# Softmax sums of every second j tile added up by accumulating DMAs, with one product with ones for them, in a four-layer graph network kernel

## The chip, the cores and the metric

The kernel runs on one core of a Trainium2 chip. The metric is device microseconds for one execution, and a time is the median of several runs. Times of the trace come from one further execution, taken with the hardware profiler. Engines are named as the profile names them: PE is the matrix engine (PEld its weight loads), DVE the vector engine, ACT the activation engine, POOL the GpSimd engine, SP the engine that issues nearly all DMAs.

## What is computed

Four layers over `x` of shape (8, 2048, 128), with one adjacency matrix of 2048 x 2048 for all. Layers 0 and 3 are graph attention with one head, layer 2 is a mean over neighbours. The change lies in layer 1, masked attention with four heads of 32:

```python
q = (x @ W_q).reshape(Bn, Nn, NUM_HEADS, HEAD_DIM).transpose(0, 2, 1, 3)
...
scores = jnp.einsum('bhnd,bhmd->bhnm', q, k) / np.sqrt(HEAD_DIM).astype(np.float32)
scores = jnp.where(adj == 0, -jnp.inf, scores)
attn = jax.nn.softmax(scores, axis=-1)
out = jnp.einsum('bhnm,bhmd->bhnd', attn, v)
out = out.transpose(0, 2, 1, 3).reshape(Bn, Nn, NUM_HEADS * HEAD_DIM)
return out @ W_o + b_o
```

The kernel does not divide the weights. It forms e = exp(score + shift) x mask, sums e x v and e alone over all j, and divides at the end. The sums of e alone are the "softmax sums" of the title.

## The kernel before

**Tiles of the attention.** Columns of a weight tile are 256 targets i, its partitions 128 sources j. A block is (b, ib, jp): batch b of 8, one of 8 groups of 256 targets, one of 8 pairs of j tiles; 512 blocks in all, jp innermost. A block goes through four functions:

- `scores` (L1017): for each of its 2 j tiles and 4 heads, one product of 32 x 128 keys with 32 x 256 queries, into two PSUM tiles. A float32 product is two instructions on PE, so the trace shows 16 a block.
- `exponentials` (L1035): two ACT instructions over 1,024 elements a partition write the tile `e`, laid out as head, j tile, target. `e` comes from the pool `ep` with 4 buffers of 8 KB a partition.
- `masked_weights` (L1043): two DVE instructions multiply `e` by the 0/1 mask in place.
- `values` (L1053): for each j tile, four products (one a head, in its own 32 columns of PE) of the values with `e` into `acc[:, 0, :]`, and four of a tile of ones with `e` into `acc[:, 1, :]`. Both sums accumulate in PSUM over the 16 j tiles of a (b, ib). L1063 is the line of both.

After jp = 7, `finished` (L1072) takes the reciprocal of `acc[:, 1, :]` (L1079), multiplies (L1081) and goes through `wo`.

**Order.** PE, DVE, ACT and POOL run in the order in which the program issues instructions. `block_steps` gives each block six steps: scores in step 0, exponentials in step 1, loads ahead in step 2, masks in step 3. In step 0 of block n, after its scores, come the values of block n-2. These steps are the main list. Other work is woven between them: by `work`, in proportion to given weights, and by `locked`, which sets three main steps beside each step of a graph attention loop. The other work is layer 0 of a batch ahead, layers 2 and 3 of the batch behind, and the norms and projections before the attention. So the distance from one block to the next differs from stretch to stretch.

**POOL's queue.** POOL has the roots of the norms (L356, L357), which DVE or ACT wait for when they apply a norm (L364, L372, L379), the node weights (L606), and the scaling of the graph attention's values (`gat_values`, L496, four steps of four instructions each). It issues no DMA before the change.

**SP's queue.** SP issues the loads in program order: masks `mh` of the attention (512 KB each, L1011), keys, values and queries (L1001, L1003, L1007), masks and rows of the graph attentions (L508, L517), x, and stores. A DMA that has to wait for a buffer or for its data holds back those behind it.

**Adjacency tiles.** Before the attention, `load_adj` (L1166) takes its 16 tiles of 1 MB from the pool `ep` too; `neighbours` (L1177) reads one and then loads the one four tiles on.

Of the kernel before, what the change touches and what calls it, by code (L numbers as in the profile page):

```python
# [15 lines left out]
AF = mybir.ActivationFunctionType  # L16
ALU = mybir.AluOpType
AX = mybir.AxisListType

P = 128  # L20
# [13 lines left out]
NH = 4  # L34
HD = 32
# [3 lines left out]
def fast_path(  # L39
# [34 lines left out]
    nc = tc.nc  # L74
    B, N, F = x.shape
    T = N // P
# [3 lines left out]
    def pool(name, bufs, **kw):  # L80
        return ctx.enter_context(tc.tile_pool(name=name, bufs=bufs, **kw))
# [2 lines left out]
    xp = pool("xp", 12)  # L84
    kp = pool("kp", 6)
    qp = pool("qp", 2)
    ep = pool("ep", 4)
    op = pool("op", 1)
    mp = pool("mp", 3)
    mtp = pool("mtp", 3)  # L90
# [17 lines left out]
    def new(pool_, tag, s, shape, dt=F32):  # L108
        count[0] += 1
        return pool_.tile(list(shape), dt, tag=tag, name=f"{s}_{count[0]}")  # L110
# [58 lines left out]
    ones = const.tile([P, HD], F32, name="ones")  # L169
# [25 lines left out]
    def load_row(name, ap):  # L195
# [21 lines left out]
        out=rows[2 * T + 2 : 2 * T + 4], in_=a3.rearrange("(c f) o -> c (f o)", c=2)  # L217
# [374 lines left out]
    def layer0_ahead(b, eng=nc.gpsimd):  # L592
# [73 lines left out]
        for g in range(G):  # L666
            steps.add(0.3, lambda g=g: values(g))
# [31 lines left out]
    attn, ready, shifts = {}, {}, {}  # L699
# [226 lines left out]
    def layer3(b):  # L926
# [43 lines left out]
        for g in range(G):  # L970
            pre.add(0.3, lambda g=g: values(g))
# [41 lines left out]
    IB, JP = N // 256, T // 2  # L1013
    blocks = [(b, ib, jp) for b in range(B) for ib in range(IB) for jp in range(JP)]
    SUB = 6

    def scores(blk):  # L1017

        b, ib, jp = blk["at"]
        c0 = (ib % 2) * 256  # L1020
        blk["sc"] = psum("sc", (P, 2, 2, 256), n=2)
        held[0] += 2
        for c in range(2):
            j = 2 * jp + c
            for h in range(NH):
                r = slice(h * HD, (h + 1) * HD)
                nc.tensor.matmul(  # L1027
                    blk["sc"][h // 2][:, h % 2, c, :],
                    keys[b, j // 4][r, (j % 4) * P : (j % 4 + 1) * P],
                    queries[b, ib // 2][r, c0 : c0 + 256],  # L1030
                    start=True,
                    stop=True,
                )

    def exponentials(blk):  # L1035
        e = blk["e"] = new(ep, "e", "e", (P, NH, 2, 256))
        for a in range(2):
            nc.scalar.activation(  # L1038
                e[:, 2 * a : 2 * a + 2], blk["sc"][a], AF.Exp, bias=shifts[blk["at"][0]]
            )  # L1040
        held[0] -= 2

    def masked_weights(blk):  # L1043
        b, ib, jp = blk["at"]
        c0 = (ib % 2) * 256
        k = 2 * jp % 8
        m = masks[b, ib // 2, jp // 4][:, k : k + 2, c0 : c0 + 256]
        m = m.unsqueeze(1).to_broadcast([P, 2, 2, 256])
        for a in range(2):
            e = blk["e"][:, 2 * a : 2 * a + 2]  # L1050
            nc.vector.tensor_tensor(e, e, m, ALU.mult)  # L1051

    def values(blk):  # L1053
        b, ib, jp = blk["at"]
        if jp == 0:
            state["acc"] = new(psa, "acc", "acc", (P, 2, 256))
        acc = state["acc"]
        for c in range(2):
            j = 2 * jp + c
            for s in range(2):  # L1060
                for h in range(NH):
                    r = slice(h * HD, (h + 1) * HD)
                    nc.tensor.matmul(  # L1063
                        acc[r, s, :],
                        ones if s else vals[b, j // 4][:, j % 4, r],
                        blk["e"][:, h, c, :],
                        start=(j == 0 and s == 0),
                        stop=(j == T - 1),
                        skip_group_check=True,
                    )  # L1070

    def finished(blk):  # L1072

        b, ib, _ = blk["at"]
        acc, ao = state.pop("acc"), {}

        def weigh():
            ao["rec"] = new(op, "rec", "rec", (P, 256))
            nc.vector.reciprocal(ao["rec"], acc[:, 1, :])  # L1079
            ao["T"] = new(op, "aoT", "aoT", (P, 256))  # L1080
            nc.vector.tensor_tensor(ao["T"], acc[:, 0, :], ao["rec"], ALU.mult)  # L1081

        def measured():
            k = b * IB + ib
            nc.scalar.activation(
                ao["rec"], ao["rec"], AF.Copy, accum_out=sums[:, k : k + 1]
            )

        def back():
            pw = psum("pwo", (P, 2, P))  # L1090
            for t in range(2):
                nc.tensor.matmul(
                    pw[:, t, :], ao["T"][:, t * P : (t + 1) * P], wo, start=True, stop=True
                )
            k = 2 * (ib % 2)
            xg = xs[b][ib // 2][:, k : k + 2, :]
            ao["last"] = later(lambda: nc.vector.tensor_tensor(xg, pw, xg, ALU.add))

        def wait():
            pass  # L1100

        return [weigh, measured] + [wait] * 5 + [back, wait, wait, lambda: settle(ao["last"])]

    def prefetch(n):
        b, ib, jp = blocks[n]
        g = ib // 2
        if n == 0:
            for k in range(G):
                load_keys(0, k)
            load_queries(0, 0)  # L1110
            for k in range(2):
                load_masks(0, 0, k)
        nb, ng = (b, g + 1) if g + 1 < G else (b + 1, 0)
        if ib % 2 == 1 and nb < B:
            if jp == 2:
                load_masks(nb, ng, 0)
                load_queries(nb, ng)
            if jp == 5:
                load_masks(nb, ng, 1)
            if nb > b:  # L1120
                if jp == 2:
                    load_keys(nb, 0)
                if jp >= 2 and jp % 2 == 0:
                    load_keys(nb, jp // 2)

    state = {}
    going = {}

    def block_steps(n):

        blk = {}

        def sub(s):
            def go():
                if s == 0:
                    if n < len(blocks):
                        if n == 0:
                            prefetch(0)
                        blk["at"] = blocks[n]
                        going[n] = blk  # L1140
                        scores(blk)
                    if n >= 2 and n - 2 < len(blocks):
                        old = going.pop(n - 2)
                        values(old)
                        if old["at"][2] == JP - 1:
                            pending.extend(finished(old))
                elif s == 1 and n < len(blocks):
                    exponentials(blk)
                elif s == 2 and 0 < n < len(blocks):
                    prefetch(n)  # L1150
                elif s == 3 and n < len(blocks):
                    masked_weights(blk)
                if pending:
                    pending.pop(0)()

            return go

        return [sub(s) for s in range(SUB)]
# [84 lines left out]
    with tc.manual_schedule(engines=ENGINES):  # L1243
# [10 lines left out]
        n = 12  # L1254
# [107 lines left out]
        for b in range(B):  # L1362
# [10 lines left out]
            if b + 1 < B:  # L1373
                xs[b + 1] = []
                loop0 = layer0_loop(b + 1, sts[b + 1])
                n = -6 if b else len(side)
# [6 lines left out]
                if loop3:  # L1383
# [4 lines left out]
                    n = len(loop0) - 4  # L1388
# [320 lines left out]
def gnn_kernel(tc, x, *others):  # L1709

    nc = tc.nc
    B, N, F = x.shape
    T, G = N // P, N // 512
    with ExitStack() as ctx:
        dr = ctx.enter_context(tc.tile_pool(name="dr", bufs=1, space=bass.MemoryType.DRAM))
        fl = ctx.enter_context(tc.tile_pool(name="fl", bufs=1))

        mt_all = [dr.tile([P, T, 512], FP8, tag=f"mt{g}", name=f"mt_all{g}") for g in range(G)]
        mg_all = [
            dr.tile([P, T, n * P], FP8, tag=f"mg{k}", name=f"mg_all{k}")  # L1720
            for k, (_, n) in enumerate(GROUPS)
        ]
        dv_all = dr.tile([T, P], F32, tag="dv", name="dv_all")
        hb_all = [dr.tile([P, 4, P], F32, tag=f"hb{g}", name=f"hb_all{g}") for g in range(G)]
        kept = (mt_all, mg_all, dv_all, hb_all)
        within = fl.tile([P, 2 * B], F32, name="within")
        flag = fl.tile([1, 1], F32, name="flag")
        fast_path(tc, kept, within, flag, x, *others)
        least = fl.tile([1, 1], F32, name="least")
        nc.vector.tensor_reduce(least, within[0:1, :], AX.X, ALU.min)  # L1730
        nc.vector.tensor_tensor(least, least, flag, ALU.min)
        usual = fl.tile([1, 1], I32, name="usual")
        nc.vector.tensor_copy(usual, least)
        v = nc.values_load(usual[0:1, 0:1], min_val=0, max_val=1)
        with tc.If(v == 0):
            general_path(tc, kept, x, *others)
# [52 lines left out]
```

## Time and profile before

| | us |
|---|---|
| median of 3 runs (3563.13 to 3566.41) | 3564.96 |
| the profiled execution | 3572.35 |
| its span, first to last instruction | 3570.5 |
| first and last start of L1063 | 216.9 to 3415.1 |
| DVE before its masks, idle until ACT's exponentials (209 times) | 304.1 |
| ACT before its exponentials, idle until PE's scores (326 times) | 452.9 |
| PE before its scores, idle until ACT's exponentials (8 times) | 14.1 |
| POOL before L356, idle until DVE's statistics (101 times) | 1486.6 |

Mean granted TensorE clock 0.962; DMA 82 GB/s on average. In the page, a group's row gives the line, the engine, the operation, output and inputs by name, the shapes and the count; behind the bar stand the busy time, the mean of one in ns, and the engine's idle time just before with what ended it. PE's busy time is modelled, and the four heads of a group run beside each other in PE's columns, so a mean of one product is longer than its share of the time. The chain of waits is followed back from the last instruction, at each step to what released it. A timeline row gives start, duration, engine, line and a run of like instructions.

### The profile page before, as it was taken

The page shows a single profiled execution, that of the slowest core. Times are in us where ns is not written, and L with a number is a line of the kernel's source. Part 1 is how long each engine was busy: PE and PEld are TensorE (multiplying, and loading weights), DVE is VectorE, ACT ScalarE, POOL GpSimd, SP SyncE. Part 2 cuts the span into 40 slices and gives each one's busy share as a digit, 9 for nine tenths or more (in the row PEclk, how much of TensorE's full clock was granted, in tenths as well). Part 3 has the DMA queues.
Part 4 walks back from the last instruction along what each step waited for, and adds up shares of the span by engine and source line. Part 5 has one row for each costly group of instructions (what it writes and reads, how often), then busy time and mean ns, then how long its engine had stood idle before and what let it go on. Part 6 is the DMA issues. An engine that isn't in the chain of part 4 may idle for free.

```text
span 3570.5 us, 85981 instructions
## 1 busy us (share of the span) xinstructions
PE 3253.6 (91%) x36367; PEld 2339.9 (66%) x36367; DVE 2684.5 (75%) x4933; ACT 2596.0 (73%) x3969; POOL 774.8 (22%) x717
## 2 busy tenths in 40 slices
PE   4789988999999999999999999999999999999987
PEld 3656654676766766676766767577676776655767
DVE  6668767677867878588795787768785887857755
ACT  4667756777876778777877687767787677676766
POOL 1032023111431115113241023311142120103011
PEclk7989988999999999999999999999999999999989
DMA  8511121213231132311323132221323112130132
GB/s 295 169 57 56 38 89 50 86 46 109 70 103 54 47 114 83 105 39 57 105 78 102 47 102 71 91 69 49 116 69 115 41 52 94 59 105 31 47 111 59
DMA packets 185190, 292.91 MB, mean 82 GB/s; under 512 B 36647, under 2 KB 99805, under 8 KB 182749
## 3 DMA queue, kind: packets, MB, share of 16 engines
q1 hardware_dynamic: 184288, 287.12, 25.4%
q8 instruction: 288, 4.72, 0.5%
q14 instruction: 106, 0.86, 0.1%
q10 hardware_dynamic: 508, 0.22, 0.0%
HBM read 235.75 MB, written 51.52 MB: 80 GB/s over the span
## 4 chain that ended last, share of the span: by engine, by line
PE 58%; DVE 27%; ACT 10%; issue 3%; POOL 1%; DMA 1%; SPq 0%; ACTq 0%; DVEq 0%; POOLq 0%
PE gacc L548 17%; PE acc L1063 17%; PE sc L1027 11%; DVE e L1051 9%; PE pagg L869 7%; DVE ge L537 5%; ACT ge L532 3%; ACT e L1038 3%; DVE ln_s L348 2%; DVE rec L1079 2%; DVE h L364 2%; ACT h L379 1%; PE ptr L390 1%; PE pqk L724 1%; PE ph L404 1%
## 5 line engine op out<-in xcount | busy, mean ns | idle before, releaser
L1051 DVE TENSOR_TENSOR e<-e,mh 128x1024 f32<-128x1024 f32 x1024 | 1208.6, 1222 | 304.3 <-ACT e L1038 304.1
L1038 ACT ACTIVATE e<-sc,shift 128x1024 f32<-128x1024 f32 x1024 | 1082.8, 1109 | 457.4 <-PE sc L1027 452.9
L548 PE MATMUL gacc<-va,ge 128*128 128x129 f32 x8192 | 1040.4, 281 | 127.7 <-DVE ge L537 66.4
L548 PEld LDWEIGHTS gacc<-va,ge 128*128 128x128 f32 x8192 | 966.7, 194 | 257.5 <-issue 140.8
L532 ACT ACTIVATE ge<-ab,gnf,gt 128x384 f32<-128x384 f32 (+1 forms) x1536 | 905.8, 666 | 27.6 <-DMA ab<-rowd 19.3
L537 DVE SCALAR_TENSOR_TENSOR ge<-ge,gnf,mg 128x768 f32<-128x768 f32 (+1 forms) x768 | 692.8, 931 | 47.1 <-ACT ge L532 40.0
L1027 PE MATMUL sc<-qr,ks 32*128 32x256 f32 x8192 | 650.5, 412 | 65.0 <-ACT e L1038 14.1
L1063 PE MATMUL acc<-e,vs 128*32 128x256 f32 x8192 | 663.9, 396 | 6.8 <-DVE aoT L1081 5.7
L1063 PE MATMUL acc<-e,ones 128*32 128x256 f32 x8192 | 649.3, 389 | 0.0
L1027 PEld LDWEIGHTS sc<-qr,ks 32*128 32x128 f32 x8192 | 403.3, 188 | 193.8 <-issue 41.8
L356 POOL TENSOR_SCALAR ln_r<-ln_mv 128x4 f32<-128x4 f32 x128 | 117.9, 921 | 1494.4 <-DVE ln_mv L350 1486.6
L1063 PEld LDWEIGHTS acc<-e,vs 128*32 128x32 f32 x8192 | 219.2, 111 | 280.2 <-issue 179.3
L1063 PEld LDWEIGHTS acc<-e,ones 128*32 128x32 f32 x8192 | 273.2, 113 | 188.5 <-issue 20.8
L860 ACT CAST mr<-mt 128x512 fp32r<-128x512 fp8e4 x512 | 272.2, 619 | 48.3 <-PE pagg L869 45.5
L869 PE MATMUL pagg<-mr,hm 128*128 128x512 f32 x1024 | 259.0, 407 | 12.2 <-ACT mr L860 6.8
L869 PEld LDWEIGHTS pagg<-mr,hm 128*128 128x128 f32 x1024 | 180.3, 190 | 86.0 <-ACT mr L860 45.3
L357 POOL TENSOR_TENSOR ln_r<-ln_r,neg_half 128x4 f32<-128x4 f32 x128 | 208.5, 1629 | 10.7
L1079 DVE RECIPROCAL rec<-acc 128x256 f32<-128x256 f32 x64 | 112.3, 1755 | 108.5 <-PE acc L1063 108.5
L493 POOL COPY va<-gv 128x16 f32<-128x16 f32 x15 | 3.2, 213 | 733.4 <-ACT gv L471 733.4
L889 DVE TENSOR_TENSOR agT<-pagg,dv 128x512 f32<-128x512 f32 x32 | 22.1, 691 | 158.8 <-PE pagg L869 151.0
L496 POOL TENSOR_SCALAR va<-va,gv 128x128 f32<-128x128 f32 x128 | 133.9, 1065 | 0.0
L390 PE MATMUL ptr<-ident,h 128*128 128x128 f32 x512 | 92.2, 300 | 42.8 <-DVE h L364 30.6
(168 smaller groups left out, 2273.9 us busy)
## 6 DMA issues: line engine op xcount, KB each, us to landing
mg<-mg_all SPq DMA_DIRECT2D x128, 384.0 KB, 3.2
mh<-mt_all SPq DMA_DIRECT2D x64, 512.0 KB, 3.8
mt<-mt_all SPq DMA_DIRECT2D x64, 512.0 KB, 3.9
adj<-in_adj_dram SPq DMA_DIRECT2D x16, 1024.0 KB, 7.8
mg<-mg_all SPq DMA_DIRECT2D x64, 256.0 KB, 2.9
ab<-rowd SPq DMA_DIRECT2D x64, 192.0 KB, 3.2
h<-in_x_dram SPq DMA_DIRECT2D x32, 256.0 KB, 3.0
x<-in_x_dram SPq DMA_DIRECT2D x32, 256.0 KB, 2.9
```

The source lines that it names most:

```text
L357: nc.gpsimd.tensor_tensor(r, r, neg_half[:, 0:4], ALU.pow)
L496: eng.tensor_scalar(va[:, j, 0:P], h[:, k, :], st["v"][:, j : j + 1], None, ALU.mult)
L532: nc.scalar.activation(e[:, c, :], gr[k]["rho"], AF.Relu, bias=st["nf"], scale=t)
L537: nc.vector.scalar_tensor_tensor(e, e, st["nf"], mt, ALU.subtract, ALU.mult)
L548: nc.tensor.matmul(gr[k]["acc"][:, q, :], e[:, c, q * P : (q + 1) * P], st["va"][:, j, :], start=(j == 0 and q == 0), stop=(j == T - 1), s ...
L860: nc.scalar.copy(t, st["mt", g, j // 8][:, j % 8, :])
L869: nc.tensor.matmul(st["pa"], st["hm"][:, j, s, :], m, start=(j == 0 and s == 0), stop=(j == T - 1 and s == 1), skip_group_check=True,)
L1027: nc.tensor.matmul(blk["sc"][h // 2][:, h % 2, c, :], keys[b, j // 4][r, (j % 4) * P : (j % 4 + 1) * P], queries[b, ib // 2][r, c0 : c0 + ...
L1038: nc.scalar.activation(e[:, 2 * a : 2 * a + 2], blk["sc"][a], AF.Exp, bias=shifts[blk["at"][0]])
L1051: nc.vector.tensor_tensor(e, e, m, ALU.mult)
L1063: nc.tensor.matmul(acc[r, s, :], ones if s else vals[b, j // 4][:, j % 4, r], blk["e"][:, h, c, :], start=(j == 0 and s == 0), stop=(j == ...
L1079: nc.vector.reciprocal(ao["rec"], acc[:, 1, :])
```

## The change

The tile `e` is laid out as j tile, head, target, so that one j tile's four heads are 4 KB in one piece on each partition. For the blocks with jp below 7, the second j tile's weights no longer meet the ones on PE. A new function adds them, after the mask, into one SBUF tile a (b, ib): SP copies the first, and for jp 1 to 6 POOL issues DMAs that add to the tile. In the block with jp = 7 both j tiles still meet the ones, and after them four products of ones with the added-up tile close the sum. A new pool `sp` holds two such tiles of 4 KB a partition, and `ep` has 3 buffers in place of 4. The new function is called in step 5 of each block.

```diff
-    ep = pool("ep", 4)
+    ep = pool("ep", 3)
+    sp = pool("sp", 2)
...
     def exponentials(blk):
-        e = blk["e"] = new(ep, "e", "e", (P, NH, 2, 256))
+        e = blk["e"] = new(ep, "e", "e", (P, 2, NH, 256))
         for a in range(2):
             nc.scalar.activation(
-                e[:, 2 * a : 2 * a + 2], blk["sc"][a], AF.Exp, bias=shifts[blk["at"][0]]
+                e[:, :, 2 * a : 2 * a + 2, :].rearrange("p c h i -> p h c i"),
+                blk["sc"][a], AF.Exp, bias=shifts[blk["at"][0]],
             )
...
-        m = m.unsqueeze(1).to_broadcast([P, 2, 2, 256])
+        m = m.unsqueeze(2).to_broadcast([P, 2, 2, 256])
         for a in range(2):
-            e = blk["e"][:, 2 * a : 2 * a + 2]
+            e = blk["e"][:, :, 2 * a : 2 * a + 2, :]
             nc.vector.tensor_tensor(e, e, m, ALU.mult)
+
+    def added(blk):
+        b, ib, jp = blk["at"]
+        if jp == JP - 1:
+            return
+        e = blk["e"][:, 1].rearrange("p h i -> p (h i)")
+        if jp == 0:
+            adds[b, ib] = new(sp, "adds", "adds", (P, NH * 256))
+            nc.sync.dma_start(out=adds[b, ib], in_=e)
+        else:
+            nc.gpsimd.dma_start(out=adds[b, ib], in_=e, accum_op=ALU.add)
...
             for s in range(2):
+                if s and c and jp < JP - 1:
+                    continue
                 for h in range(NH):
...
-                        blk["e"][:, h, c, :],
+                        blk["e"][:, c, h, :],
                         start=(j == 0 and s == 0),
-                        stop=(j == T - 1),
+                        stop=(j == T - 1 and s == 0),
                         skip_group_check=True,
                     )
+        if jp == JP - 1:
+            a = adds.pop((b, ib))
+            for h in range(NH):
+                nc.tensor.matmul(
+                    acc[h * HD : (h + 1) * HD, 1, :],
+                    ones,
+                    a[:, h * 256 : (h + 1) * 256],
+                    start=False,
+                    stop=True,
+                    skip_group_check=True,
+                )
...
                 elif s == 3 and n < len(blocks):
                     masked_weights(blk)
+                elif s == 5 and n < len(blocks):
+                    added(blk)
```

More of the change, by code (lines that the diff above doesn't have):

```diff
@@ L1124, in prefetch @@
                     load_keys(nb, jp // 2)
-    state = {}
-    going = {}
+    state, going, adds = {}, {}, {}
     def block_steps(n):
```

## The prediction

> **What bounds the kernel now.** I read the shares of the engines, then the chain of waits, then the costliest groups, then the table of DMA issues, and last the timeline of a stretch in which attention runs close packed. Whole page first:
>
> ```profile
> PE 3253.6 (91%) x36367; PEld 2339.9 (66%) x36367; DVE 2684.5 (75%) x4933; ACT 2596.0 (73%) x3969; POOL 774.8 (22%) x717
> ...
> q1 hardware_dynamic: 184288, 287.12, 25.4%
> ...
> PE 58%; DVE 27%; ACT 10%; issue 3%; POOL 1%; DMA 1%; SPq 0%; ACTq 0%; DVEq 0%; POOLq 0%
> PE gacc L548 17%; PE acc L1063 17%; PE sc L1027 11%; DVE e L1051 9%; PE pagg L869 7%; DVE ge L537 5%; ACT ge L532 3%; ACT e L1038 3%; DVE ln_s L348 2%; DVE rec L1079 2%; DVE h L364 2%; ACT h L379 1%; PE ptr L390 1%; PE pqk L724 1%; PE ph L404 1%
> ...
> L1063 PE MATMUL acc<-e,vs 128*32 128x256 f32 x8192 | 663.9, 396 | 6.8 <-DVE aoT L1081 5.7
> L1063 PE MATMUL acc<-e,ones 128*32 128x256 f32 x8192 | 649.3, 389 | 0.0
> L496 POOL TENSOR_SCALAR va<-va,gv 128x128 f32<-128x128 f32 x128 | 133.9, 1065 | 0.0
> ...
> mh<-mt_all SPq DMA_DIRECT2D x64, 512.0 KB, 3.8
> ```
>
> PE is the fullest engine and the largest part of the chain that ended last, and one line of it, L1063, is what the change thins out. No DMA is in that chain (1%), the DMA engines are a quarter busy, and POOL has time. But 27% of the chain is DVE, so a shorter PE step is not a gain everywhere. Now the timeline of the stretch, PE's scores, ACT's exponentials and DVE's masks, with one stretch of POOL:
>
> ```profile
> 1830.52 17.88 POOL L496 TENSOR_SCALAR va<-h,gv 128x128 f32<-128x128 f32 x16
> ...
> 1842.93 1.15 PE L1027 MATMUL sc<-qr,ks 32*128 32x256 f32 x16
> 1844.12 2.12 ACT L1038 ACTIVATE e<-sc,shift 128x1024 f32<-128x1024 f32 x2 [0.82 <-PE sc L1027]
> 1845.69 2.32 DVE L1051 TENSOR_TENSOR e<-e,mh 128x1024 f32<-128x1024 f32 x2
> 1845.88 1.15 PE L1027 MATMUL sc<-qr,ks 32*128 32x256 f32 x16
> ...
> 1847.06 2.12 ACT L1038 ACTIVATE e<-sc,shift 128x1024 f32<-128x1024 f32 x2 [0.82 <-PE sc L1027]
> 1848.82 1.15 PE L1027 MATMUL sc<-qr,ks 32*128 32x256 f32 x16
> ...
> 1850.00 2.12 ACT L1038 ACTIVATE e<-sc,shift 128x1024 f32<-128x1024 f32 x2 [0.82 <-PE sc L1027]
> 1853.87 1.12 ACT L1038 ACTIVATE e<-sc,shift 128x1024 f32<-128x1024 f32 x1 [0.83 <-PE sc L1027]
> ```
>
> Each score row opens a block. Here blocks follow each other after 2.95 us (1842.93, 1845.88, 1848.82), while the mean over all 512 is 6.25 us, worked out from the mask rows of the whole trace (a quarter of the distances is under 4.5 us, a quarter over 7.3). So the kernel has stretches in which a block must be done in 3 to 4 us, and a chain of transfers, one a block, has to keep up with those and not with the mean.
>
> **The products with ones.** Of a block's two j tiles the second loses its four products with ones, in seven blocks of eight: 448 groups of four heads. 64 groups come back, one for each (b, ib). Net 384 of the 2,048 groups of L1063. In the close stretch a block is 2.95 us, of which scores take 1.08 (first to last score in the chain of waits), so four groups take 1.87 and one 0.467: PE loses 384 x 0.467 = 179 us of work. Not all of it is on the path. L1063 has 17% of the chain, 607 us of 3570.5; 384/2048 of that is **114 us**. Ends: 0 (DVE ends last instead) and 179. I take 114, which is what the chain itself holds.
>
> **The exponentials and masks.** Same count, same 1,024 elements; only the order of two strides differs. Over all of their rows L1038 takes 1092 to 1132 ns and L1051 1177 to 1416, median 1219. I take 0; the ends go by the wider of the two, median to shortest, 42 ns: 1024 x 0.042 = 43 us either way, on engines that are a quarter idle.
>
> **The buffers.** `ep` falls from 4 to 3. In PE's order the values of block n-3 come ahead of the scores of block n, for which the exponential waits anyway, so without the DMA the third buffer costs nothing. The adjacency tiles use the same pool: a load goes out one DVE pass later. Those passes (L1177, 16 of them, 13.0 to 97.4 us) are 5.6 us apart, a load lands after 7.8, and three passes remain between issue and need, 17 us. Cost 0; if that cover is gone, up to the 7.8 of one load, with SP's loads of constants behind it.
>
> **The copy.** At jp = 0 SP issues a 512 KB copy behind that block's mask. SP stands until DVE is there; behind it are loads of masks, keys and rows, each issued blocks ahead. SP already stands for DVE's masks (140.8 us in L1011, 28 times) without a DMA on the chain. 64 copies: 0. It lands like the mask load of the same size, 3.8 us, before the next mask is done at the mean distance.
>
> **The accumulating DMAs.** 384, issued by POOL, 512 KB each, jp 1 to 6. They form a chain: number n starts after its mask (M), and after number n-1 has landed, as both write one tile. They hold the buffer: the exponential of block n+3 must wait until number n has read e. Behind that exponential, ACT's Relu of the other attention and its PSUM reads are queued, then PE.
>
> The trace has no DMA from POOL and no accumulation, so the time L from mask to landing is bounded: below by the plain 512 KB load, **3.8 us**, which reads once what an addition must read twice; above by the slowest 512 KB in the table of DMA issues, the stores of mt_all, **8.9**. I build my value: 3.8 for the plain transfer, a second reading of 512 KB, and the issue. q1 moved 287.12 MB in 25.4% of 3570.5 us, 3.16 us a MB, so 0.524 MB hold an engine for 1.66 us. For POOL's issue the nearest row is one of its own instructions over 128 partitions, L496 with 1.07 us (SP's issue rows are 0.32). Sum **6.5 us**. By SP's issue it would be 5.8.
>
> What L does, I worked out from the trace's own times: end of each mask pair, start of each exponential pair. An accumulation starts at the later of its mask and its forerunner's landing; where it lands after the exponential three blocks on (or the last after the closing product, 1 us behind that block's exponential), everything later is shifted by as much. By hand in the stretch above: the mask ends at 1848.01, the exponential three blocks on starts at 1853.87 (its own is at 1844.12), so 5.86 us are there, and with 6.5 already the first is 0.6 late, each next one more, 3.5 a block. In the mean block the room is 13.8 us (median); 10% of the blocks have less than 6.5. Shifts over the whole kernel: L = 3.8: 7 us; 4.5: 40; 5.5: 104; 6: 141; **6.5: 192**; 7: 258; 8: 433; 9: 720; 10: 1045. It is rigid: other work that fills a wait is not counted, nor is the closer packing by a faster PE, and I let these two stand against each other.
>
> By the Trainium skill (DMA: Bandwidth & Descriptors, Anatomy of one DMA) a transfer issued from POOL takes 2.0 us plus its bytes at 436 GB/s, and by Collectives: The Full Stack (the part on why ReduceScatter is half of AllGather) an addition is dear for its two source reads alone. That estimates 2.0 + 2 x 1.2 = 4.4 us, 34 us of shifts, and a kernel 80 us faster. No run here shows it; the 3.8 us that a plain load takes is near the page's 3.2.
>
> Against the change speaks another page of the skill, SBUF — State Buffer (Who interferes with whom, and the trap "DVE blocks DMA" ahead of it): descriptors of a DMA from the GpSimd queue are written by those cores, which are shut out while DVE runs copies or tensor_scalars in a two-port mode; the page has 620 ns growing to 3100. Nothing in this trace shows it. By it L would be an estimated 2.5 us longer where such an instruction falls on the issue, and at 6.5 + 2.5 = 9 throughout, 720 us of shifts would make 4171.
>
> **POOL's queue.** 384 issues of 1.07 are 411 us beside 775: not full. But POOL works in order. Behind a waiting accumulation stand the roots of the norms (L356, L357), for which DVE's L364 and L372 wait, now only 25 us in all; as long as L keeps below the distance of blocks they wait no longer. The other way, an accumulation stands behind the 16 L496, 17.88 us at 1830.52, in some 15 places. Those are four steps spread over about 10 us of blocks, so one behind them is about 8 us late against 13.8 - 6.5 = 7.3 of room: I take 0; at the far end 17.9 - 7.3 = 10.6, 159 us in all.
>
> **DMA load.** 64 copies of 1.66 and 384 accumulations of 1.66 to 3.31 add 743 to 1,377 us, 21 to 39% of the engines' time, to 46 to 64%. Loads come blocks ahead; 0.
>
> **Sum.** 3572.35 (the profiled run; span 3570.5, 1.85 around it) - 114 + 192 = 3650. That execution is 7.4 above the median of 3564.96, so **3643** beside it: slower by 2.2%.
>
> **Rivals.**
> A. *The chain keeps up* (L under 5.7, where shifts are 114). For it: a plain load lands after 3.8, a store of 256 KB from SBUF after 2.0 to 2.4, against 2.9 for the load, so SBUF sources may be quicker. Against: three numbers must all be at their low end. At L = 4.5: 3565 - 114 + 40 = 3491; at best, 3.8 and the whole 179, 3393.
> B. *The addition is dear of itself* (L over 8): the accumulation chain becomes the bound nearly everywhere. Place: the exponential's wait for a buffer; decides from 8 us on. For it: the 8.9 of the stores, and the other transfers beside it. Against: rows of 4 KB, the kindest shape. L = 9: 3565 - 114 + 720 = 4171; L = 12: 1,800 of shifts, above 5,200.
> C. *It makes no difference*: the saved time goes to DVE's 27% and ACT's 10%, and the chain is hidden: 3565. For it, DVE's 75%; against, PE is busy for all of 1840 to 1860, the close stretch.
>
> **Chances.** About 0.2%, 7 us, is what can be told from no change. Forecast case (L 5.7 to 8, 3570 to 3885, likeliest 3643) 0.38; A 0.36; B 0.22; C 0.04. Faster is A, 0.36; within is C and a sliver at L = 5.7, 0.05; slower 0.59. The range: of A only what lies under 3460 is left out, some 0.04 (L near 3.8 and over 114 saved), of B what lies over 4180 (L over 9), some 0.15: 3460 to 4180. The likeliest case's own range is 3570 to 3885.
>
> **What will show it.** Products with ones: 8192 - 448 x 8 = 4608 rows on the old line and 64 x 8 = 512 on the new one. POOL's DMA issues with their landing: 6.5 right, under 5.7 A, over 8 B. ACT's exponentials waiting for a DMA or for POOL (none now); PE's scores, 65 us idle now, waiting for ACT. In the close stretch, blocks at L's distance instead of 2.95. Wrong it would be if L is long and no exponential waits, if POOL's roots hold DVE first, or if L1038 or L1051 changes its mean.

## The result and the profile after

The changed kernel takes 3665.94 us (median of 4 runs, 3651.86 to 3670.06) beside 3564.05 for the kernel before: ratio 1.0282, 95% interval 1.025 to 1.0314. It is slower by 102 us, where 79 were forecast. The lines of its page that answer to those shown of before:

```profile
PE 3170.3 (87%) x33295; PEld 2280.1 (62%) x33295; DVE 2686.7 (73%) x4933; ACT 2594.4 (71%) x3969; POOL 1064.8 (29%) x1101
...
q0 software_dynamic: 55296, 201.35, 29.7%
q1 hardware_dynamic: 193504, 320.67, 27.0%
...
L1039 ACT ACTIVATE e<-sc,shift 128x1024 f32<-128x1024 f32 x1024 | 1081.9, 1108 | 544.9 <-PE sc L1028 232.7
L1053 DVE TENSOR_TENSOR e<-e,mh 128x1024 f32<-128x1024 f32 x1024 | 1209.3, 1222 | 349.8 <-ACT e L1039 349.0
...
L1064 POOL DMA_DIRECT2D adds<-e x384 | 344.0, 896 | 2117.0 <-DVE e L1053 995.7
...
L1028 PE MATMUL sc<-qr,ks 32*128 32x256 f32 x8192 | 695.3, 420 | 132.5 <-ACT e L1039 81.6
...
L1078 PE MATMUL acc<-e,ones 128*32 128x256 f32 x4608 | 371.1, 394 | 0.0
...
adds<-e POOLq DMA_DIRECT2D x384, 512.0 KB, 4.9
...
adds<-e SPq DMA_DIRECT2D x64, 512.0 KB, 2.9
```

Lines of the changed kernel are numbered a little higher: its L1028 is the L1027 of before, L497 the L496, L1078 the L1063, and L1089 is the closing product. The work is as the change has it: 4,608 products with ones on the old line, 384 additions from POOL. PE has 83 us less to do, ACT and DVE the same as before, and the span is still 90 us longer. So the time went into waits: PE's scores now stand for ACT's exponentials (81.6 us, 14.1 before), and ACT's exponentials for something new. Here are the scores of before, from the page, and a wait of before to which the list below has a counterpart:

```profile
L1027 PE MATMUL sc<-qr,ks 32*128 32x256 f32 x8192 | 650.5, 412 | 65.0 <-ACT e L1038 14.1
```

```profile
DVE h L364 <- POOL ln_r L357: 12.2, 7, 7.0
```

The list of waits of the changed kernel (engine and line, who was waited for, us in all, times, longest) names it:

```profile
POOL adds L1064 <- DMA adds<-e: 560.6, 123, 9.7
...
ACT e L1039 <- DMA adds<-e: 176.6, 57, 8.1
...
DVE h L365 <- POOL ln_r L358: 58.5, 32, 8.3
```

An addition waits at POOL for its forerunner's landing 123 times, an exponential for an addition 57 times, and DVE, applying a norm, waits for POOL's roots 58.5 us in place of 12.2.

**Where.** The last mask of each (b, ib) in the trace gives the time that each of the 64 rows took. The 14 rows in which blocks follow each other closely (26 to 42 us each before, but for the first, which holds the start) are ib 0 of all batches, ib 1 and 2 of the first, and ib 1, 2, 4, 5 of the last.

| us up to the last mask | before | changed | change |
|---|---|---|---|
| the 14 close rows (the first with the start) | 705.5 | 818.8 | +113.3 |
| the other 50 rows | 2704.0 | 2674.2 | -29.9 |
| after the last mask | 161.0 | 168.1 | +7.2 |

The row ib 0 of the other seven batches is 35.1 us before (mean), 46.2 after. Here is one of them, batch 5, in the changed kernel's timeline, POOL alone:

```profile
2299.84 7.11 POOL L497 TENSOR_SCALAR va<-h,gv 128x128 f32<-128x128 f32 x8
2306.90 0.92 POOL L1064 DMA_DIRECT2D adds<-e  x1
2307.55 10.37 POOL L497 TENSOR_SCALAR va<-h,gv 128x128 f32<-128x128 f32 x8
2317.87 0.89 POOL L1064 DMA_DIRECT2D adds<-e  x1
2322.98 0.86 POOL L1064 DMA_DIRECT2D adds<-e  x1 [4.22 <-DMA adds<-e]
2328.04 0.86 POOL L1064 DMA_DIRECT2D adds<-e  x1 [4.20 <-DMA adds<-e]
2328.61 0.57 POOL L357 TENSOR_SCALAR ln_r<-ln_mv 128x4 f32<-128x4 f32 x1
...
2333.12 0.93 POOL L1064 DMA_DIRECT2D adds<-e  x1 [2.81 <-DMA adds<-e]
```

and ACT's exponentials and DVE's masks and norms in the same stretch:

```profile
2310.52 2.12 ACT L1039 ACTIVATE e<-sc,shift 128x1024 f32<-128x1024 f32 x2 [1.81 <-issue]
2313.49 2.12 ACT L1039 ACTIVATE e<-sc,shift 128x1024 f32<-128x1024 f32 x2 [0.85 <-DMA adds<-e]
2322.55 2.12 ACT L1039 ACTIVATE e<-sc,shift 128x1024 f32<-128x1024 f32 x2 [6.94 <-DMA adds<-e]
2327.62 2.12 ACT L1039 ACTIVATE e<-sc,shift 128x1024 f32<-128x1024 f32 x2 [2.95 <-DMA adds<-e]
...
2307.95 2.44 DVE L1053 TENSOR_TENSOR e<-e,mh 128x1024 f32<-128x1024 f32 x2
...
2330.35 1.11 DVE L365 TENSOR_SCALAR h<-x,ln_mv,ln_r 128x128 f32<-128x128 f32 x4 [4.29 <-POOL ln_r L358]
```

Read it in order. The mask that starts at 2307.95 ends at 2310.39, but its addition is issued only at 2317.87, because POOL first works off eight L497. Part of these 7.5 us it would have waited anyway: its forerunner, issued at 2306.90, had landed by 2313.4, which lets the exponential at 2313.49 go. The other 4.5 us are POOL's. The exponential three blocks on stands until 2322.55, when that addition has landed. From there a link of the chain takes 5.1 us (2317.87, 2322.98, 2328.04, 2333.12), and blocks, which came 3 us apart (2310.52, 2313.49), come at that pace (2322.55, 2327.62). The root L357 at 2328.61 is issued behind the addition that waited until 2328.04, and DVE's norm waits for it 4.29 us. Three waits then come from one queue: the exponential's for its buffer, DVE's for a root, and the addition's for POOL's other work.

### The profile page after: what moved, and what is told of

Read it like the earlier page. It is cut to its first block, busy times and chain, and to the rows that moved or that the text cites. A ratio compares the mean times of both kernels' runs of the same rounds, so it can differ in the third digit from the quotient of the medians.

```text
span 3661.0 us, 81445 instructions
## 1 busy us (share of the span) xinstructions
PE 3170.3 (87%) x33295; PEld 2280.1 (62%) x33295; DVE 2686.7 (73%) x4933; ACT 2594.4 (71%) x3969; POOL 1064.8 (29%) x1101
## 3 DMA queue, kind: packets, MB, share of 16 engines
q0 software_dynamic: 55296, 201.35, 29.7%
## 5 line engine op out<-in xcount | busy, mean ns | idle before, releaser
L1039 ACT ACTIVATE e<-sc,shift 128x1024 f32<-128x1024 f32 x1024 | 1081.9, 1108 | 544.9 <-PE sc L1028 232.7
L1053 DVE TENSOR_TENSOR e<-e,mh 128x1024 f32<-128x1024 f32 x1024 | 1209.3, 1222 | 349.8 <-ACT e L1039 349.0
L549 PE MATMUL gacc<-va,ge 128*128 128x129 f32 x8192 | 1062.5, 285 | 187.6 <-DVE ge L538 91.6
L549 PEld LDWEIGHTS gacc<-va,ge 128*128 128x128 f32 x8192 | 987.2, 197 | 324.6 <-issue 145.2
L1064 POOL DMA_DIRECT2D adds<-e x384 | 344.0, 896 | 2117.0 <-DVE e L1053 995.7
L1028 PE MATMUL sc<-qr,ks 32*128 32x256 f32 x8192 | 695.3, 420 | 132.5 <-ACT e L1039 81.6
L1078 PE MATMUL acc<-e,vs 128*32 128x256 f32 x8192 | 667.3, 398 | 4.2 <-DVE aoT L1107 2.7
L1028 PEld LDWEIGHTS sc<-qr,ks 32*128 32x128 f32 x8192 | 423.7, 192 | 288.4 <-ACT e L1039 118.7
L1078 PEld LDWEIGHTS acc<-e,vs 128*32 128x32 f32 x8192 | 220.4, 112 | 282.6 <-issue 178.0
L1078 PE MATMUL acc<-e,ones 128*32 128x256 f32 x4608 | 371.1, 394 | 0.0
L1078 PEld LDWEIGHTS acc<-e,ones 128*32 128x32 f32 x4608 | 155.2, 114 | 108.9 <-issue 16.3
L357 POOL TENSOR_SCALAR ln_r<-ln_mv 128x4 f32<-128x4 f32 x128 | 138.3, 1080 | 275.4 <-DVE ln_mv L351 267.9
L358 POOL TENSOR_TENSOR ln_r<-ln_r,neg_half 128x4 f32<-128x4 f32 x128 | 194.0, 1516 | 10.7
L365 DVE TENSOR_SCALAR h<-x,ln_mv,ln_r 128x128 f32<-128x128 f32 x384 | 106.7, 344 | 58.5 <-POOL ln_r L358 58.5
```

What stands on the lines that cost most here:

```text
L358: nc.gpsimd.tensor_tensor(r, r, neg_half[:, 0:4], ALU.pow)
L549: nc.tensor.matmul(gr[k]["acc"][:, q, :], e[:, c, q * P : (q + 1) * P], st["va"][:, j, :], start=(j == 0 and q == 0), stop=(j == T - 1), s ...
L1028: nc.tensor.matmul(blk["sc"][h // 2][:, h % 2, c, :], keys[b, j // 4][r, (j % 4) * P : (j % 4 + 1) * P], queries[b, ib // 2][r, c0 : c0 + ...
L1039: nc.scalar.activation(e[:, :, 2 * a : 2 * a + 2, :].rearrange("p c h i -> p h c i"), blk["sc"][a], AF.Exp, bias=shifts[blk["at"][0]],)
L1064: nc.gpsimd.dma_start(out=adds[b, ib], in_=e, accum_op=ALU.add)
L1078: nc.tensor.matmul(acc[r, s, :], ones if s else vals[b, j // 4][:, j % 4, r], blk["e"][:, c, h, :], start=(j == 0 and s == 0), stop=(j == ...
```

## The experiments

Each run is compared with runs of the kernel before taken beside it on the same chip; its difference is to those. Before was 3565.55 us beside the layout, the saving, the copies and the half chain; 3571.86 beside the half chain with L497 on DVE, the selected rows, and the chain from jp = 1 with three and with four buffers; 3565.70 beside the last four.

**The layout and the third buffer alone.** The products with ones all back, no DMA:

```diff
-                if s and c and jp < JP - 1:
-                    continue
...
-                elif s == 5 and n < len(blocks):
-                    added(blk)
```

> All products with ones are back on PE and nothing is added by DMA; what stays of the change is the new order of e (j tile, head, target) and the pool of three buffers, which the adjacency tiles share. Theory (the loss comes from the accumulating transfers): the time of before, 3564, with L1038's and L1051's means (1109 and 1222 ns before) unchanged, within 7 us. Rival (strides or the third buffer cost): 3580 to 3660, with a longer mean of the exponentials or masks, or exponentials that wait for a buffer.

3573.26, ratio 1.0022 (1.0012 to 1.0032): 8 us slower. The means of exponentials (1109) and masks are as before, and no exponential waits for a buffer. A cost just over the bound, where 0 was taken; what it is was not traced further.

**The saving alone.**

```diff
-            a = adds.pop((b, ib))
+            a = blk["e"][:, 1].rearrange("p h i -> p (h i)")
...
-                elif s == 5 and n < len(blocks):
-                    added(blk)
```

> The second j tile's products with ones are left out in seven blocks of eight as in the changed kernel, no DMA adds them up, and the closing four products read the last block's own e in place of the added-up tile: PE's work is that of the changed kernel, the second tiles' share of the softmax sums is left out. It prices the saving alone. Theory: 114 us as the prediction took it, 3450 (ends 3385 for the full 179 and 3565 for none). If the saving is only 20 to 40 us, the transfers cost far less than thought (about 130), if it is 150 or more they cost about 250 in all.

3516.38, ratio 0.9857 (0.9841 to 0.9873): 49 us faster than before. The new layout and the three buffers are in this run too; against the run ahead, which differs from it in the products alone, it is 57 us faster. That is half of the 114. The chain of waits of this run tells why:

```profile
PE 47%; DVE 36%; ACT 10%; issue 3%; POOL 3%; DMA 1%; SPq 0%; ACTq 0%; POOLq 0%; DVEq 0%
PE gacc L548 15%; DVE e L1052 13%; PE acc L1077 10%; PE sc L1027 9%; DVE ge L537 7%; PE pagg L869 6%; ACT e L1038 4%; ACT ge L532 3%; DVE rec L1104 3%; DVE ln_s L348 3%; DVE h L364 2%; DVE hp L678 1%; PE ph L404 1%; PE pqk L724 1%; DVE ln_mv L350 1%
```

PE's share fell from 58 to 47% and DVE's rose from 27 to 36%, its masks from 9 to 13%: where PE got shorter, DVE ended last. The transfers of the changed kernel thus cost 102 + 49, about 151 us; the layout's 8 are in both runs and not among them. Of the 146 us between the two profiled spans 111 lie in the 14 close rows, 26 in the other 50.

**Copies in place of additions.**

```diff
-            nc.gpsimd.dma_start(out=adds[b, ib], in_=e, accum_op=ALU.add)
+            nc.gpsimd.dma_start(out=adds[b, ib], in_=e)
```

> POOL's DMAs of jp 1 to 6 copy in place of adding (the sums then lack all but the last of them); same sizes, same queue, same waits, but one reading less. Theory (time from issue to landing is what counts, 4.9 us in the changed kernel): landing falls to 3 to 4 us, the chain to about 4 us a link, and most of the shifts go: 3480 to 3540. Rival (the place in POOL's in-order queue, descriptor writing, or waiting roots cost): landing shorter, but the time stays at 3630 to 3670.

3584.33, ratio 1.0054 (1.0037 to 1.0071): 19 us slower than before, 68 over the saving alone. Its page and its waits:

```profile
q0 software_dynamic: 55296, 201.35, 14.2%
...
adds<-e POOLq DMA_DIRECT2D x384, 512.0 KB, 3.1
```

```profile
POOL adds L1064 <- DMA adds<-e: 143.4, 40, 7.5
...
ACT e L1039 <- DMA adds<-e: 87.5, 30, 7.1
```

The same bytes, queue and order, but a landing of 3.1 us in place of 4.9 takes away 83 of the 151 us. The number expected was too low because it held the 114; that the landing counts is shown. The 68 that are left are hardly a cost of POOL's DMAs as such: nearly all of them lie in the close rows (765.4 us, 707.6 with the saving alone; the others 2649.2 and 2648.1), where a copy too can be late.

**Half the chain.**

```diff
-        if jp == JP - 1:
+        if jp % 2:
             return
...
-                if s and c and jp < JP - 1:
+                if s and c and jp % 2 == 0:
                     continue
```

> Only the blocks with even jp give their second j tile to the DMAs: one copy and three additions a (b, ib) in place of one and six, 192 groups of products saved in place of 384. The chain then has two blocks for each link. Theory (chain too slow for close stretches): nearly no shifts, half the saving: 3505 to 3550, faster than before. Rival (each addition costs by itself, by POOL's time or by DMA traffic): half of the loss of the changed kernel, about 3615.

3592.13, ratio 1.0076 (1.0059 to 1.0093): 27 us slower. If half the saving is some 25, the 192 additions cost about 51 us. In this run POOL waits only 25.1 us for a landing, so the chain itself is no longer late; yet exponentials wait 56.0 us for additions, 11 times, up to 9.4. By the trace, seven of the 11, each of 6.8 us or more, are for an addition that POOL issued right after its L497; they make 50 of the 56.0. The expectation missed this: the queue costs without a chain.

**Half the chain, L497 of layer 0 on DVE.**

```diff
-            gat_values(st, hv(g), g, eng)
+            gat_values(st, hv(g), g, nc.vector)
```

> The half chain of the earlier run (even jp alone, 3592), with layer 0's scaling of the values (16 instructions of L497 a batch, 17.9 us together on POOL) moved to DVE, where one takes 0.28 us. In the half chain no link waits for its forerunner, and the exponential waits fall right behind those 16 in seven places of 6 to 9 us. Theory (POOL's order makes an addition late there): those waits go, DVE takes 7 x 4.5 = 31 us more work of which part is on the path; 3545 to 3575. Rival (the additions themselves): 3592 plus what DVE adds, 3595 to 3620.

3573.64, ratio 1.0009 (1.0 to 1.0019), 2 us above before and 25 below the half chain, by the differences. The exponentials' wait for additions falls, from the first of these rows to the second:

```profile
ACT e L1039 <- DMA adds<-e: 56.0, 11, 9.4
```

```profile
ACT e L1039 <- DMA adds<-e: 15.7, 9, 4.8
```

So in the half chain POOL's own work ahead of an addition was most of the loss.

**Only rows that leave room.**

```diff
+    def thin(b, ib):
+        return ib not in {0: (0, 1, 2), B - 1: (0, 1, 2, 4, 5)}.get(b, (0,))
...
-                if s and c and jp < JP - 1:
+                if s and c and jp < JP - 1 and thin(b, ib):
                     continue
```

> The DMAs add only in the rows (b, ib) whose blocks leave them room: left as before (all products with ones on PE) are ib 0 of every batch, ib 1 and 2 of the first, and ib 1, 2, 4, 5 of the last, 14 of 64 rows; the other 50 rows are those of the changed kernel. By the times at which a row's last mask ends, these 14 rows hold 120 of the loss, and the rest holds a saving of some 40 us against before. Theory (the loss sits in the close stretches): 3525 to 3550, faster than before, and hardly an exponential that waits for a DMA. Rival (each addition costs by itself): 50/64 of the loss of 102, about 3645.

3561.82 beside 3571.86, ratio 0.9966 (0.9952 to 0.998): 10 us faster than the kernel before, with 300 of the 384 additions still made. 22% fewer additions take 112 us off. The gain was less than forecast (the table above has the loss of the 14 rows at 113 and the saving of the others at 30, not 120 and 40). The other rows return part of the saving: they take 2679.0 us, against 2648.1 with the saving alone. And the 14 rows, which add nothing here, take 719.3 in place of 705.5; why was not traced. Exponentials now wait for additions 18.0 us:

```profile
POOL adds L1067 <- DMA adds<-e: 375.4, 80, 9.6
...
ACT e L1039 <- DMA adds<-e: 18.0, 10, 4.0
```

The chain still waits for itself (375.4), but in these rows hardly anything else waits for the chain. That a wait is long says nothing of what it costs.

**The chain started at jp = 1, and with a fourth buffer.** The first is the second's control:

```diff
-        if jp == JP - 1:
+        if jp in (0, JP - 1):
             return
...
-        if jp == 0:
+        if jp == 1:
...
-    kp = pool("kp", 6)
-    ep = pool("ep", 3)
-    sp = pool("sp", 2)
+    kp = pool("kp", 5)
+    ep = pool("ep", 3)
+    sp = pool("sp", 1)
```

> The row's chain starts at jp = 1 (SP's copy) and adds at jp 2 to 6; the second j tile of jp = 0 meets the ones on PE again, one tile for the sums is enough, and the pool of keys and values has 5 buffers in place of 6. It saves 320 groups of products in place of 384 and is the control for the next run, which has a fourth e buffer. Theory: five additions a row in place of six, in the close rows some 5 us less of a stall each, 3600 to 3640. Rival (a free copy, no chain): 3655 or more.

> As the run before it, with four e buffers in place of three, so that an exponential waits for the addition of four blocks back. Theory (the wait for a buffer is where the chain costs): in a close row the room grows by one block of 3 to 4 us, some 14 rows lose 4 to 9 us less, and the time falls by 60 to 110 us against the run before, to 3520 to 3570. Rival (POOL's queue, DMA traffic or the closing product hold PE): no more than 20 us less than the run before.

3669.36 (ratio 1.0278, 1.0261 to 1.0296) with three buffers, 3664.54 (1.0263, 1.0246 to 1.028) with four: both where their rivals were put. The five buffers for keys and the single tile were not priced apart. Five links a row in place of six helped little, and the fourth buffer some 5 us, with intervals of the ratios that overlap. Waits of the run with three buffers, then of that with four:

```profile
ACT e L1039 <- DMA adds<-e: 163.3, 48, 9.2
...
DVE h L365 <- POOL ln_r L358: 59.9, 34, 9.5
...
PE ptr L391 <- DVE h L365: 39.2, 15, 7.5
```

```profile
DVE h L365 <- POOL ln_r L358: 91.8, 33, 12.9
PE ptr L391 <- DVE h L365: 91.3, 16, 15.1
...
ACT e L1039 <- DMA adds<-e: 55.2, 15, 6.6
...
PEld acc L1089 <- DMA adds<-e: 47.7, 15, 8.2
PE acc L1089 <- DMA adds<-e: 40.0, 15, 7.7
```

The buffer's wait fell by 108 us, and two others took its place: DVE for POOL's roots, with PE's transposes behind it, and the closing products for the last addition. The theory that the exponential's wait for a buffer is *the* place falls. It is only the first of three at which a late chain is felt.

**Two chains, and POOL's L497 away.** Additions go by turns to two tiles, so a link waits for the landing two blocks back:

```diff
-            adds[b, ib] = new(sp, "adds", "adds", (P, NH * 256))
-            nc.sync.dma_start(out=adds[b, ib], in_=e)
+            adds[b, ib, k] = new(sp, f"adds{k}", "adds", (P, NH * 256))
+            nc.sync.dma_start(out=adds[b, ib, k], in_=e)
...
-            nc.gpsimd.dma_start(out=adds[b, ib], in_=e, accum_op=ALU.add)
+            nc.gpsimd.dma_start(out=adds[b, ib, k], in_=e, accum_op=ALU.add)
```

> Additions go in turn to two tiles (odd and even jp): copies at jp 1 and 2, additions at 3 to 6, two closing sets of products; 256 groups saved, about 38 us by the saving measured. A link now waits for the landing two blocks back, so a chain takes two blocks' time for its 5.05 us. Theory (links that wait for their forerunner set the pace in the close rows): the stalls left are those behind L497 on POOL, 3580 to 3615, and POOL's wait for a landing falls from 560 us to under 100. Rival (POOL's order or the additions' own cost): as with the single chain started at jp 1, 3650 or more.

> Two chains, and layer 0's scaling of the values moved from POOL to DVE. Theory (landing and POOL's L497 are the two causes): both gone, 3540 to 3575, row ib 0 of the middle batches at 37 to 39 us in place of 47. Rival: something else of the additions is left, 3600 or more.

> The changed kernel with one chain, layer 0's scaling of the values on DVE. Prices POOL's L497 by itself. Theory: the close rows start without the backlog, the chain still loses 5.05 less 3.5 us a block there: 3600 to 3640. If POOL's order is all, about 3540; if it is nothing, 3665 or more.

> The kernel before with layer 0's scaling of the values on DVE: the control for the two runs ahead of it. Seven batches have 16 instructions of 0.28 us, 31 us of DVE work, and POOL's roots come free 17.9 us earlier. Theory: part of the DVE work is on the path, 3565 to 3585. Rival: POOL's place was on the path before, 3550.

| | us | ratio to before | interval |
|---|---|---|---|
| one chain (changed kernel) | 3665.94 | 1.0282 | 1.025 to 1.0314 |
| one chain, L497 of layer 0 on DVE | 3630.42 | 1.0185 | 1.0166 to 1.0203 |
| two chains | 3580.75 | 1.0035 | 1.0021 to 1.005 |
| two chains, L497 of layer 0 on DVE | 3589.47 | 1.0067 | 1.0045 to 1.0089 |
| before, L497 of layer 0 on DVE | 3574.63 | 1.0023 | 1.0012 to 1.0033 |

Two chains save a third less work on PE, and lose 15 us in place of 102. Fewer additions alone do not do that: the 192 of the half chain lose 27. POOL's wait for a landing all but goes, and with it the others; of the two-chain run:

```profile
ACT e L1039 <- DMA adds<-e: 40.1, 21, 8.9
...
DVE h L365 <- POOL ln_r L358: 31.1, 26, 8.7
...
POOL adds L1065 <- DMA adds<-e: 16.8, 4, 6.1
```

Moving L497 costs 9 us by itself. With one chain it brings 37 (102 to 65), so POOL's backlog there was worth about 46; with two chains it brings nothing beyond its own 9. The expectation for the latter missed. Room to catch up is not the whole reason, as the half chain had it too and gained 25. With two chains SP copies at jp = 1 and 2, and POOL's first addition of a row comes at jp = 3, not 2 as in the half chain: an exponential's waits for additions issued right behind L497 are 1.5 to 3.5 us in the middle batches there, 6.8 in the half chain. Which of the two counts was not tested apart. The 14 close rows take 733.0 us with two chains (818.8 with one, 705.5 before), the other 50 rows 2690.3.

## Why the prediction was right

The time, the side and the mechanism were right; of three terms, two were mis-sized and one that was taken at 0 was not 0. That 79 forecast comes near 102 measured is in part luck: the saving was taken 57 us too large (114, measured 57), the cost of the transfers 41 too large (192, measured 151), and the two errors cancel but for 16.

- **The mechanism**: additions that form a chain, which the close stretches cannot wait for. Shown by breaking it (two chains, 87 us less than the changed kernel, 82 less than the single chain from jp = 1, each by its own difference to before), by shortening its link (copies, 83 us less), and by sparing the close rows (112 us less, faster than before). The prediction's rule for the shifts can be worked again on the times of before, now with the measured time of every addition, from the later of its mask and its forerunner's landing to its own landing, POOL's queue included. It gives 139 us for the changed kernel, where the runs have 151; 64 for the copies (68); 47 for the half chain (51). This is an estimate, as rigid as the first; it puts 132 of the 139 in the close rows, where the profiles show 111.
- **The saving**: 114 us from the chain's share; measured 57, or 49 with the layout's cost. The step that failed is to take a line's share of the chain of waits as what its shortening brings. The working had the rival, DVE at 27% of the chain, and it decided over half.
- **L**: 6.5 us forecast, of 3.8, 1.66 and 1.07. In the trace an addition is issued 0.3 us behind its mask at the soonest and lands 4.9 after its issue (median; 4.5 to 10.0), 5.2 in all; a link in the close stretch is 5.1. Over all 384, from the later of mask and forerunner to the landing, the median is 5.7 and the mean 6.0. POOL's issue, taken at 1.07, was 0.90, and the landing is counted from the issue's start, so it already holds it. The plain transfer inside SBUF lands after 3.1 from POOL and 2.9 from SP, in place of the 3.8 of a load, and the addition adds 1.8. By the prediction's own signs ("6.5 right, under 5.7 A") the landing spoke for rival A: at a constant 5.2 its rule gives 84 us of shifts, not 192, and with the 114 a kernel faster than before. It was slower because the saving was half and because not every addition took 5.2. Rival A's support was read from two rows: stores of 256 KB landed after 2.0 and 2.4, but four other rows of them (qd, kd, vd, hb_all) after 2.9 to 3.1.
- **The DMA load**, taken at 0: the 31 additions with no other transfer beside them landed after 4.5 to 4.7 us; the 60 slowest, over 6.2, had on average 2.2 us of other packets on each DMA engine in the first 4.9 us, the 128 quickest 0.3.
- **POOL's queue**: taken at 0, with 159 at the far end. The step that failed is "those are four steps spread over about 10 us": eight L497 ran between two additions for 10.37 us. In seven rows (ib 2 of the first batch, ib 0 of six others) an addition was issued right after them, 4.5 to 6.6 us after mask and forerunner were both there. About 46 us by the run without them (37, and the 9 that moving them costs in the kernel before, if it costs the same here). Roots held behind additions are a second part; it shows in DVE's 58.5 us, and was not priced by itself. With the 84 of the rule at 5.2 the 46 make 130 of 151 us; whether the two simply add, and what the rest is, stays open.
- **The wait's place**: the exponential, as said, but not alone; with a fourth buffer the root and the closing product held as much.
- **Costs taken at 0**: the masks and exponentials kept their means (1222 and 1108 ns); SP's copy landed after 2.9 us; loads took longer (the 384 KB masks 5.3 us in place of 3.2), but no engine waits more than 8 us longer in all for a load than before. The layout and third buffer cost 8 us together.

Two rules weighed ahead can now be held against rows. A plain 512 KB transfer from POOL lands after 3.1 us in the row; the estimate from the fit in the Trainium skill (DMA: Bandwidth & Descriptors, Anatomy of one DMA) was 3.2. An addition lands after 4.9; the estimate with the two source reads of Collectives: The Full Stack (the part on why ReduceScatter is half of AllGather) was 4.4. In engine time the two reads fit closely: additions held the 16 engines for 29.7% of 3661.0 us, copies for 14.2% of 3576.0, 2.83 and 1.32 us each, 2.1 times. Of the trap in SBUF — State Buffer there is no sign: of 384 issues the longest took 2.03 us, the median 0.86, and the slow landings go with other transfers and not with DVE's copies and tensor_scalars (0.17 us of them beside the 60 slowest, 0.31 beside the 128 quickest).

## What to carry to other kernels

Work moved from a full engine to a chain of transfers has to keep up with the closest stretch of the schedule, not with its mean: find the blocks that follow each other fastest and set the link's latency against them. The chain into one tile went one link at a time here (5.1 us each), and its waits sat in POOL's queue, where they held back what came behind them (DVE's wait for POOL's roots rose from 12.2 to 58.5 us); two tiles by turns, or sparing the close stretches, took away most of the loss here. And a line's share of the chain of waits can be far above what its shortening brings (114 against 57 us here), since another engine may stand ready to end last.

## What was not expected of the hardware

The granted TensorE clock fell with the waits, from 0.962 before to 0.947 in the changed kernel. In the stretch shown, by 20 us windows of the changed kernel (us, busy time of each engine, then granted clock, DMA share, GB/s):

```profile
2300.00:2320.00 20.00, 17.59 (x236) 11.34 (x228) 17.75 (x36) 10.53 (x14) 18.76 (x18) 1.00 0.49 126
2320.00:2340.00 20.00, 13.56 (x128) 7.18 (x128) 10.59 (x24) 9.64 (x11) 7.76 (x10) 0.74 0.57 115
```

The same products before and after a wait of PE in that stretch:

```profile
2310.83 0.61 PE L1078 MATMUL acc<-e,ones 128*32 128x256 f32 x8
...
2323.72 2.08 PE L1028 MATMUL sc<-qr,ks 32*128 32x256 f32 x12 [5.87 <-ACT e L1039]
...
2326.58 1.08 PE L1078 MATMUL acc<-e,ones 128*32 128x256 f32 x8
```

Eight products took 0.61 us ahead of the wait of 5.87 us and 1.08 behind it; the granted clock was 1.00 from 2310 to 2320, 0.58 from 2320 to 2325 and 0.74 from 2325 to 2330. So here a stall was paid for again in slower products after it. How much of the 151 us that is was not measured apart.
